# Sandwich layer, one core: three of four heads' probabilities turned by VectorE and moved through DRAM, shared weights resident, one lasting tile for table rows, zeros written one block per step

## The chip, the cores and the metric

The kernel runs on 1 core of one Trainium2 chip. The metric is device time in microseconds (us), the median of 3 runs. A profile of one execution is read beside it. Engines are named as in the profile: PE is TensorE's matmul side and PEld its weight loads, DVE is VectorE, ACT is ScalarE, POOL is GpSimd, and SP is SyncE, which issues most DMAs.

## What is computed

Input x has 8 sequences of 512 rows of 512 numbers, all f32. Two blocks follow each other, each of the form x + norm(block(norm(x))), where norm is a layernorm without weights. The reference, cut to what matters:

```python
c_kv, c_q = x @ W_DKV + b_DKV, x @ W_DQ + b_DQ            # latent 128
k_c, v_c, q_c = c_kv @ W_UK + b_UK, c_kv @ W_UV + b_UV, c_q @ W_UQ + b_UQ
k_r, q_r = (x @ W_KR + b_KR) * pe, (x @ W_QR + b_QR) * pe  # 32 wide, shared by 16 heads
scores = (q_c k_c + q_r k_r) / sqrt(32)                    # 16 heads of 32, per sequence 512 x 512
ctx = softmax(scores) @ v_c;  attention = ctx @ W_O + b_O
# second block: 16 experts, 2 per row by a grouped top-k of sigmoid router scores
routed = sum over chosen e of weight_e * relu(x @ w_up[e])**2 @ w_down[e]   # 512 -> 256 -> 512
shared = relu(x @ shared_up)**2 @ shared_down                               # 512 -> 1024 -> 512
```

## The kernel before

The work has three stages: attention with the shared expert mixed into it, the routed experts, and a tail that adds the parts and normalizes.

**Attention.** The loop at L1094 runs over 8 sequences `b` and 16 steps `g` each. A step is one group of four heads (`m = g // 4`) and one block of 128 query rows (`qt = g % 4`). `scores(b, g)` (L345) makes four score tiles of 128 x 512 on PE. On DVE, one operation per head (L370) adds the position scores, writes the negated sum to SBUF and takes its row minimum. On ACT, L380 makes the exponentials in place. The probabilities have queries on partitions, and the weighted sum with the values needs keys there, so each must be turned. That is done in two ways:

- Heads 0 and 1, tile `p`: `keys_first` (L403) turns each on PE in four 128 x 128 transposes (L410) one step later. The result is copied out of PSUM into `pT`, head 0 by DVE (L418) and head 1 by ACT (L420).
- Heads 2 and 3, tile `pb`: `blocks` (L422) turns 32 x 32 blocks on DVE in one instruction (L427) into `pB`, of which there are two buffers. Four DMAs (L439) write `pB` to one of four DRAM buffers `turned`. In the next step `put_together` (L443) reads it back with one DMA (L446) into the tile `pTb`. The DRAM round trip moves the blocks to their partitions.

`weighted_sum` (L468) runs once per group of four steps, at the second step of the next group (g % 4 == 1), and reads the one `pT` and the one `pTb` tile (L479). The last group of the last sequence is turned wholly on PE.

**What else a step holds.** `beside(b, g)` (L1019) lists the other attention work by step: the output projection of the sequence before (g 2 and 3), its norms, router and top-k (g 4 to 10), the indirect DMAs by POOL that scatter its rows into `table` (`send`, g 11 and 12), and the first projections of the next sequence (g 6 to 15). The rest of a step is filled from the list `waiting`, items of the shared expert with written-out costs, up to BUDGET = 5.4 per step (L1015, L1105). These items begin at step 7 of sequence 1. Thirteen of the sixteen half sequences of the shared expert are done in this stage, three in the tail.

**Order.** PE's order in this stage is the order of the calls. The order on the other engines and on SP is made by a scheduler from dependencies and a model of costs. Each queue is worked off in order, so an instruction that waits holds up those behind it.

**The pieces that the change touches.**

- Shared up weights: in this stage `load_wsu` (L748) reads 512 KB pieces into two buffers `wsu` whenever a piece is due (L752). For the tail the whole 2 MB go into `wsu_all`, loaded in the middle of the routed stage (L976). `shared_down` lies in `wsd` from the start (L194).
- Table rows: `ao[b]` (L504, L541) is one tile per sequence from a pool with one buffer. It holds the attention output, then its normed rows, the 16 expert weights, a row number at NUMBER and 15 zeros. `weights` (L673) writes weights, zeros (the memset at L684) and numbers. Since the buffer is one, a write into the new tile waits for the scatters that read the tile before.
- Zeros: `none` (L113) is a tile of zeros with a row number. `clear(g)` (L731) writes it from SBUF, in sequence 0, three 256 KB blocks of `sums` and one 272 KB block of `table` in each step (L738, L739), 57 DMAs with the one at L195.

**Routed stage.** 79 tiles of 128 table rows, each with the weights of its expert (L880 and on): 272 KB of rows (`xg`) and up to 1 MB of weights per tile, three weight buffers.

Of the kernel before, what the change touches and what calls it, by code (L numbers as in the profile page):

```python
# [38 lines left out]
def sandwich_kernel(  # L39
# [65 lines left out]
    def load_rows(src, b, name):  # L105
        t = sh.tile([P, NT, D], F32, tag="x", name=f"{name}_{b}")
        for i in range(NT):
# [3 lines left out]
    xs, res = {0: load_rows(x, 0, "x")}, {}  # L111

    none = sb.tile([P, W], F32, name="none")  # L113
    nc.vector.memset(none, 0.0)
    nc.gpsimd.iota(none[:, NUMBER : NUMBER + 1], pattern=[[0, 1]], base=T, channel_multiplier=1,
                   allow_small_or_imprecise_dtypes=True)
    numbers = sb.tile([P, B * NT], F32, name="numbers")
# [76 lines left out]
    wsd = chunked(shared_down, "wsd", const)  # L194
    nc.sync.dma_start(table[NE * REGION :, :], none)  # L195
# [123 lines left out]
    def heads(b, m):  # L319
# [18 lines left out]
    rope, probs, pTs, ctxs, dens, wides, last_max = {}, {}, {}, {}, {}, {}, {}  # L338
    BLK = HEAD_DIM
    NB = P // BLK  # L340
    turned = [
        dram.tile([P, NB, 2 * NT * BLK], F32, name=f"turned_{i}") for i in range(NT)
    ]

    def scores(b, g):  # L345
# [3 lines left out]
        tiles, order = {}, (2, 3, 0, 1)  # L349
        for h in order:  # L350
# [10 lines left out]
        pr = [  # L361
            at.tile([P, 2, S], F32, tag="p", name=f"p_{b}_{g}", bufs=2),
            at.tile([P, 2, S], F32, tag="pb", name=f"pb_{b}_{g}"),
        ]
# [3 lines left out]
        for h in order:  # L368
            p_h = pr[h // 2][:, h % 2, :]
# [9 lines left out]
            )  # L379
            nc.scalar.activation(  # L380
# [7 lines left out]
        probs[b, g] = pr  # L388
# [5 lines left out]
    def turned_probs(b, m):  # L394
        if (b, m) not in pTs:
            pTs[b, m] = (
                at.tile([P, 2, NT, S], F32, tag="pT", name=f"pT_{b}_{m}"),

                at.tile([P, NT * NB, 2, NT, BLK], F32, tag="pTb", name=f"pTb_{b}_{m}"),
            )  # L400
        return pTs[b, m]

    def keys_first(b, g, hs):  # L403

        m, qt = divmod(g, NT)
        for h in hs:
            pr = probs[b, g][h // 2][:, h % 2, :]
            pt = ps_o.tile([P, NT, P], F32, tag="o", name=f"pt_{b}_{g}_{h}")
            for c in range(NT):
                nc.tensor.transpose(pt[:, c, :], pr[:, c * P : (c + 1) * P], ident)  # L410
            to = turned_probs(b, m)[h // 2]
            if h < 2:
                to = to[:, h, :, qt * P : (qt + 1) * P]
            else:
                to = to[:, qt * NB : (qt + 1) * NB, h - 2].rearrange("p i c q -> p c i q")
                pt = pt.rearrange("p c (i q) -> p c i q", q=BLK)
            if h % 2 == 0:
                nc.vector.tensor_copy(to, pt)  # L418
            else:
                nc.scalar.copy(to, pt)  # L420

    def blocks(b, g):  # L422


        pr = probs[b, g][1]
        pB = at.tile([P, NB, 2, NT, BLK], F32, tag="pB", name=f"pB_{b}_{g}", bufs=2)
        turn = nc.vector.transpose(  # L427
            pB.rearrange("p j h c q -> p (h c) j q"),
            pr.rearrange("p h (c j q) -> p (h c) j q", j=NB, q=BLK),
        )  # L430
        tc.add_manual_dep(
            turn.ins,
            last_max.pop((b, g)).ins.name,
            mybir.DependencyInfo(mybir.DependencyClass.NoSync, mybir.DependencyReason.SCHED_ONLY),
            reason="the exponentials take a while",
        )
# [6 lines left out]
    def put_together(b, g):  # L443
        m, qt = divmod(g, NT)
        to = turned_probs(b, m)[1][:, qt * NB : (qt + 1) * NB]
        nc.sync.dma_start(to.rearrange("p i h c q -> p i (h c q)"), turned[qt])  # L446
# [12 lines left out]
    def turn_denominators(b, m, pt=None):  # L459
# [5 lines left out]
        ctxs[b, m] = at.tile([P, S], F32, tag="ctx", name=f"ctx_{b}_{m}", bufs=5)  # L465
        nc.scalar.copy(ctxs[b, m], pt.rearrange("p t q -> p (t q)"))

    def weighted_sum(b, m, ps=None):  # L468
# [5 lines left out]
        for c in range(NT):  # L474
            for h in range(4):
# [4 lines left out]
                    to if h < 2 else to.rearrange("p (n q) -> p n q", q=BLK),  # L480
                    lhsT=vs[b][:, c, col : col + HEAD_DIM],
                    rhs=pT[:, h, c, :] if h < 2 else pTb[:, :, h - 2, c, :],
# [17 lines left out]
    ao, xT, sc_, chosen_ = {}, {}, {}, {}  # L500

    def project_out(b, i):
        if i == 0:
            ao[b] = at.tile([P, NT, W], F32, tag="ao", name=f"ao_{b}")  # L504
# [4 lines left out]
        nc.vector.tensor_tensor(ao[b][:, i, 0:D], ps, bo, ALU.add)  # L509
# [6 lines left out]
    def residual(b):  # L516

        rows = [ao[b][:, i, 0:D] for i in range(NT)]
# [7 lines left out]
    def norm_f(b):  # L526
        rstd, off = norm_stats([res[b][:, i, :] for i in range(NT)], f"f{b}")
        for i in range(NT):
            normalize(ao[b][:, i, 0:D], res[b][:, i, :], rstd, off, i)
        del res[b]  # L530

    def turn_f(b, i):
        if i == 0:
            xT[b] = sh.tile([P, NK, S], F32, tag="xT", name=f"xT_{b}", bufs=2)
        turn_rows(ao[b], xT[b], i, f"f{b}")

    def last_sequence(prev, fill):
# [3 lines left out]
        ao[b] = at.tile([P, NT, W], F32, tag="ao", name=f"ao_{b}")  # L541
# [21 lines left out]
        for i in range(NT):  # L563
            ps, row, xb = acc[i], ao[b][:, i, 0:D], res[b][:, i, :]
# [5 lines left out]
        for i in range(NT):  # L570
            turn_rows(ao[b], xT[b], i, f"f{b}")
# [101 lines left out]
    def weights(b):  # L673
        chosen = chosen_[b][1]
        comb = ao[b][:, :, D:NUMBER]
# [5 lines left out]
        nc.vector.tensor_tensor(  # L681
            comb, comb, total.unsqueeze(2).to_broadcast([P, NT, NE]), ALU.mult
        )
        nc.vector.memset(ao[b][:, :, NUMBER + 1 :], 0.0)  # L684
        nc.vector.tensor_copy(
            ao[b][:, :, NUMBER : NUMBER + 1], numbers[:, b * NT : (b + 1) * NT].unsqueeze(2)
        )

# [42 lines left out]
    def clear(g):  # L731


        assert NE == NSTEP
        todo = [(1, c) for c in range(T // P + 1)] + [(0, T // P)]
        todo += [(0, c) for c in range((2 * B - LATE) * NT // 2, B * NT)]
        for i, c in todo[g * 3 : (g + 1) * 3] if g < NSTEP - 1 else todo[g * 3 :]:
            nc.sync.dma_start(sums[i][c * P : (c + 1) * P, :], none[:, 0:D])  # L738
        nc.sync.dma_start(table[g * REGION : g * REGION + P, :], none)  # L739

    def send(b, i):
        for j in range(TOP_K):
            scatter(slots[b][:, i, j : j + 1], ao[b][:, i, :])


    hT, wsu_, ysum = {}, {}, {}

    def load_wsu(b, a, i):  # L748
        if (b, a, i) not in wsu_ and 2 * b + a < 2 * B - LATE:
            wsu = sh.tile([P, NK, INTER], F32, tag="wsu", name=f"wsu_{b}_{a}_{i}", bufs=2)  # L750
# [462 lines left out]
```

## Time and profile before

| | us |
|---|---|
| runs | 1772.99, 1770.25, 1768.58 |
| median | 1770.25 |
| the profiled execution, its own time | 1769.93 |
| its span, first to last instruction | 1768.2 |
| score matmuls of step 0 of sequence 0 begin | 33.4 |
| sequence 0, 16 steps (33.4 to 137.4) | 104.0 |
| sequences 1 to 6 | 162.0, 157.5, 159.1, 159.3, 158.5, 160.2 |
| sequence 7 and what follows, to the first routed tile (1093.9 to 1324.4) | 230.5 |
| routed stage (1324.4 to 1660.0) | 335.6 |
| tail | 108.2 |

The time around the span is 1.7 us. Stage bounds are the starts of instructions on PE's timeline: a sequence begins with the scores of its step 0. The profile gives for each engine its busy time, for each group of instructions a count and a mean duration, and for each idle stretch of an engine who ended it ("<-"). A busy PE is not a PE at its peak: at a granted clock of 0.5 the same matmul takes twice as long and counts as busy.

### The profile page before, as it was taken

To read this page: it belongs to the slowest core of one execution; us is meant where nothing else is said; L and a number is where in the kernel's file an instruction comes from. 1 tells how busy PE (TensorE), PEld (TensorE's weight loads), DVE (VectorE), ACT (ScalarE), POOL (GpSimd) and SP (SyncE) were. 2 spreads that over 40 slices of the span, in tenths; PEclk is the share of its full clock that TensorE was granted. 3 is DMA by queue.
4 is the path that set the end of the run, shared out by engine and by line. 5 is a ranking of instruction groups with operands and counts; after the bars stand their busy time and mean duration, and the time that the engine had idled before them with its cause. 6 is when DMAs were issued, how large, how long until landed. Compare 5 with 4: busy or idle time off the path is not lost. (4 is left out here: it accounts for less than half of the span.)

```text
span 1768.2 us, 25701 instructions
## 1 busy us (share of the span) xinstructions
PE 1602.3 (91%) x8122; PEld 931.8 (53%) x8122; DVE 991.2 (56%) x2929; ACT 820.5 (46%) x1943; POOL 227.9 (13%) x210
## 2 busy tenths in 40 slices
PE   7788789899997998898989989999989998999995
PEld 3333554454554445444554545466457676776663
DVE  3766755765585568457755746775333332333366
ACT  4656645564564556455644645565312222222134
POOL 0000010001000100100010010002013333333222
PEclk9889899989998999898999989999999999999998
DMA  6987574446454645645564566464156978979898
GB/s 202 292 295 221 155 227 129 146 145 224 143 173 140 212 141 177 196 143 151 156 215 129 162 189 185 136 189 155 53 183 129 243 139 201 232 138 288 222 310 171
DMA packets 210728, 324.33 MB, mean 183 GB/s; under 512 B 22945, under 2 KB 126369, under 8 KB 210593
## 3 DMA queue, kind: packets, MB, share of 16 engines
q1 hardware_dynamic: 189696, 275.76, 50.3%
q0 software_dynamic: 20896, 46.93, 13.7%
q8 instruction: 65, 1.06, 0.3%
q14 instruction: 71, 0.57, 0.1%
HBM read 237.93 MB, written 142.36 MB: 215 GB/s over the span
## 5 line engine op out<-in xcount | busy, mean ns | idle before, releaser
L380 ACT ACTIVATE pb<-pb,nmax 128x512 f32<-128x512 f32 x256 | 182.8, 715 | 285.0 <-DVE nmax L370 282.1
L768 PE MATMUL h<-xT,wsu 128*128 128x256 f32 x832 | 214.0, 414 | 57.0 <-DMA wsu<-in_L_ffn_shared_up_dram 40.6
L783 PE MATMUL y<-wsd,hT 128*128 128x512 f32 x512 | 235.2, 609 | 12.1 <-DVE nmax L370 6.4
L370 DVE CUSTOM_DVE_ANT_0 pb<-s,rope 128x512 f32<-128x512 f32 x256 | 167.1, 687 | 132.9 <-PE s L353 131.1
L768 PEld LDWEIGHTS h<-xT,wsu 128*128 128x128 f32 x832 | 170.1, 209 | 99.4 <-issue 24.2
L380 ACT ACTIVATE p<-p,nmax 128x512 f32<-128x512 f32 x256 | 181.2, 709 | 2.0 <-DVE nmax L370 1.7
L410 PEld LDWEIGHTS pt<-ident,p 128*128 128x128 f32 x1024 | 110.3, 141 | 110.8 <-issue 37.2
L926 PE MATMUL hg<-xgT,set_up 128*128 128x128 f32 x1264 | 156.7, 277 | 12.1 <-DMA set_up<-in_L_ffn_w_up_dram 11.8
L370 DVE CUSTOM_DVE_ANT_0 p<-s,rope 128x512 f32<-128x512 f32 x256 | 167.1, 684 | 0.9 <-PE s L353 0.9
L783 PEld LDWEIGHTS y<-wsd,hT 128*128 128x128 f32 x512 | 96.9, 195 | 128.4 <-issue 101.9
L353 PE MATMUL s<-k,q 32*128 32x512 f32 x1024 | 157.5, 657 | 1.0 <-ACT q L329 1.0
L926 PEld LDWEIGHTS hg<-xgT,set_up 128*128 128x128 f32 x1264 | 148.5, 193 | 16.8 <-issue 8.9
L427 DVE STREAM_TRANSPOSE pB<-pb 128x1024 f32<-128x1024 f32 x124 | 153.3, 1236 | 6.1 <-ACT pb L380 4.8
L950 POOL DMA_INDIRECT sums<-y,to x79 | 122.6, 1551 | 236.1 <-DVE y L949 194.9
L410 PE MATMUL pt<-ident,p 128*128 128x128 f32 x1024 | 142.6, 281 | 7.5 <-DVE ctx L486 4.6
L941 PE MATMUL yg<-set_down,hgT 128*128 128x512 f32 x316 | 148.5, 593 | 0.0
L453 POOL COPY wide<-rden 128x512 f32<-128x512 f32 x32 | 19.7, 615 | 905.3 <-DVE rden L451 532.9
L479 PE MATMUL o<-pTb,v 128*32 128x512 f32 x496 | 118.3, 621 | 12.8 <-issue 7.0
L935 DVE TENSOR_TENSOR hgT<-hgT 128x256 f32<-128x256 f32 x79 | 33.6, 425 | 164.4 <-ACT hgT L934 164.4
L479 PE MATMUL o<-pT,v 128*32 128x512 f32 x496 | 120.7, 621 | 0.3 <-DVE pT L418 0.2
L420 ACT COPY pT<-pt 128x512 f32<-128x512 f32 x128 | 72.8, 568 | 102.3 <-PE pt L410 102.3
L911 ACT COPY xgT<-pt_g 128x512 f32<-128x512 f32 x79 | 46.2, 586 | 145.8 <-PE pt_g L909 145.7
(222 smaller groups left out, 2167.7 us busy)
## 6 DMA issues: line engine op xcount, KB each, us to landing
turned<-pB SPq DMA_DIRECT2D x496, 128.0 KB
pTb<-turned SPq DMA_DIRECT2D x124, 512.0 KB
set_up<-in_L_ffn_w_up_dram SPq DMA_DIRECT2D x79, 512.0 KB
set_down<-in_L_ffn_w_down_dram SPq DMA_DIRECT2D x79, 512.0 KB
wsu<-in_L_ffn_shared_up_dram SPq DMA_DIRECT2D x52, 512.0 KB
xg<-table SPq DMA_DIRECT2D x79, 272.0 KB
end<-sums SPq DMA_DIRECT2D x32, 512.0 KB
sums<-none SPq DMA_DIRECT2D x40, 256.0 KB
```

Of the source, the lines that this page charges most:

```text
L353: nc.tensor.matmul(tiles[h], lhsT=q[r0 : r0 + HEAD_DIM, qt * P : (qt + 1) * P], rhs=k[r0 : r0 + HEAD_DIM, :], start=True, stop=True,)
L370: last_max[b, g] = nc.vector.tensor_tensor_reduce(out=p_h, in0=tiles[h], in1=rope[b, qt], scale=-1.0, scalar=3.0e38, op0=ALU.add, op1=ALU.min,
L380: nc.scalar.activation(p_h, p_h, AF.Exp, bias=nmax[:, h : h + 1], scale=-1.0, accum_out=dens[b, m][:, qt, h : h + 1],)
L410: nc.tensor.transpose(pt[:, c, :], pr[:, c * P : (c + 1) * P], ident)
L420: nc.scalar.copy(to, pt)
L427: turn = nc.vector.transpose(pB.rearrange("p j h c q -> p (h c) j q"), pr.rearrange("p h (c j q) -> p (h c) j q", j=NB, q=BLK),)
L479: nc.tensor.matmul(to if h < 2 else to.rearrange("p (n q) -> p n q", q=BLK), lhsT=vs[b][:, c, col : col + HEAD_DIM], rhs=pT[:, h, c, :] if ...
L768: nc.tensor.matmul(ps[:, 0:HALF], lhsT=wsu[:, k, :], rhs=xT[b][:, k, a * HALF : (a + 1) * HALF], start=(k == 0), stop=(k == NK - 1),)
L783: nc.tensor.matmul(ysum[c], lhsT=hT[b][:, i, t * P : (t + 1) * P], rhs=wsd[:, i, :], start=(i == 0), stop=(i == NH - 1),)
L926: nc.tensor.matmul(ph[:, i * P : (i + 1) * P], lhsT=sets[j % NBUF][0][:, k, i * P : (i + 1) * P], rhs=xgT[j][:, k, :], start=(k == 0), sto ...
L941: nc.tensor.matmul(py, lhsT=hg[j][:, i * P : (i + 1) * P], rhs=sets[j % NBUF][1][:, i, :], start=(i == 0), stop=(i == NI - 1),)
L950: nc.gpsimd.indirect_dma_start(out=sums[j % 2][:, :], out_offset=bass.IndirectOffsetOnAxis(ap=to[j], axis=0), in_=y, in_offset=None, compu ...
```

## The change

- Heads 1, 2 and 3 (NV = 3) are turned by DVE and moved through DRAM, head 0 (NP = 1) by PE. The DVE turn is two instructions, of two heads and of one. `turned` rows grow from 1 KB to 1.5 KB, and `pTb` from 512 KB to 768 KB per step. The PE-turned head is copied by ACT, and DVE's copy goes. `pB` has one buffer in place of two.
- Hints to the scheduler (`in_order`; no wait on the chip comes of them by themselves): a step's row minima come after the step before's turn on DVE. The row number is written after the weights. A block of zeros comes after the step's `put_together`.
- `wsu` (2 MB) and `wsd` (2 MB) are both loaded in sequence 0, in steps 6 and 9, and stay. All sixteen halves of the shared expert read them. `load_wsu` and `wsu_all` are gone.
- `ao` is one lasting tile; its zeros are written once, at the start, by POOL. The memset in `weights` is gone.
- `none` is a short-lived tile that shares `pB`'s buffer. It is written to the last rows of `table`, and the zeros are copied from there, DRAM to DRAM. `clear` is a generator that gives one block per step from sequence 1 on (56 blocks, to step 7 of sequence 4).

The diff, cut:

```diff
+    BLK = HEAD_DIM
+    NB = P // BLK
+    NV = 3
+    NP = 4 - NV
-    none = sb.tile([P, W], F32, name="none")
+    none = at.tile([P, NB, NV, NT, BLK], F32, tag="pB", name="none")
+    none = none.rearrange("p j h c q -> p (j h c q)")[:, 0:W]
...
+    nc.sync.dma_start(table[NE * REGION :, :], none)
+    none = table[NE * REGION :, :]
+
+    ao = at.tile([P, NT, W], F32, name="ao")
+    nc.gpsimd.memset(ao[:, :, NUMBER + 1 :], 0.0)
...
-    wsd = chunked(shared_down, "wsd", const)
-    nc.sync.dma_start(table[NE * REGION :, :], none)
+    wsd = const.tile([P, NH, D], F32, name="wsd")
+    wsu = const.tile([P, NK, HID], F32, name="wsu")
...
-        tiles, order = {}, (2, 3, 0, 1)
+        tiles, order = {}, [*range(NP, 4), *range(NP)]
...
+            if last_turn:
+                in_order(last_max[b, g], last_turn[-1], "transfers wait for it")
...
-            if h % 2 == 0:
+            if (NP - 1 - h) % 2 == 0:
+                nc.scalar.copy(to, pt)
+            else:
                 nc.vector.tensor_copy(to, pt)
-            else:
-                nc.scalar.copy(to, pt)
...
-        pr = probs[b, g][1]
-        pB = at.tile([P, NB, 2, NT, BLK], F32, tag="pB", name=f"pB_{b}_{g}", bufs=2)
-        turn = nc.vector.transpose(
-            pB.rearrange("p j h c q -> p (h c) j q"),
-            pr.rearrange("p h (c j q) -> p (h c) j q", j=NB, q=BLK),
-        )
+        pb, last = probs[b, g][1], last_max.pop((b, g))
+        pB = at.tile([P, NB, NV, NT, BLK], F32, tag="pB", name=f"pB_{b}_{g}")
+        for h in range(0, NV, 2):
+            hs = slice(h, min(h + 2, NV))
+            turn = nc.vector.transpose(
+                pB[:, :, hs].rearrange("p j h c q -> p (h c) j q"),
+                pb[:, hs].rearrange("p h (c j q) -> p (h c) j q", j=NB, q=BLK),
+            )
+            in_order(turn, last, "the exponentials take a while")
+        last_turn.append(turn)
...
-        nc.vector.memset(ao[b][:, :, NUMBER + 1 :], 0.0)
...
+    def load_shared():
+        for w, src in ((wsu, shared_up), (wsd, shared_down)):
+            yield nc.sync.dma_start(w, src.rearrange("(c p) n -> p c n", p=P))
...
-            if j == NTILES // 2:
-                nc.sync.dma_start(wsu_all, shared_up.rearrange("(c p) n -> p c n", p=P))
...
-                    keys_first(*prev, range(2))
+                    keys_first(*prev, range(NP))
                     if by_vector(prev[0], prev[1] // NT):
-                        put_together(*prev)
+                        moved = put_together(*prev)
...
-                if b == 0:
-                    clear(g)
+
+                if (b > 0 or g in (6, 9)) and moved is not None:
+                    for ins in itertools.islice(spare, 1):
+                        in_order(ins, moved, "others are waited for")
```

## The prediction

> **What bounds the kernel now.** I read the table by stages first, then who waited for whom on PE and DVE, then the groups, then the timeline at each stall. Columns of the table by stages: stretch and its length, then busy time (and instructions) of PE, PEld, DVE, ACT, POOL, the granted clock, the DMA share, GB/s. The rows are sequence 0, sequence 4 and the routed stage.
>
> ```profile
> 33.40:137.40 104.00, 83.06 (x453) 36.87 (x452) 73.11 (x174) 66.43 (x164) 1.84 (x3) 0.89 0.83 269
> 616.00:775.20 159.20, 147.24 (x733) 77.79 (x732) 100.92 (x280) 86.29 (x208) 10.23 (x12) 0.95 0.54 168
> 1324.40:1660.00 335.60, 317.49 (x1896) 233.51 (x1895) 110.35 (x382) 77.08 (x159) 119.47 (x77) 0.99 0.85 196
> ```
>
> Sequence 4 stands for sequences 1 to 6: PE is busy 147 of 159 us, DVE 101, ACT 86, DMA at half. PE sets the pace there, so less PE work and fewer PE stalls count in full. Sequence 0 has no shared expert to fill it; PE has the most busy time but waits, and the DMA share is 0.83.
>
> The waits of PE and DVE (total us, times, longest):
>
> ```profile
> PE h L768 <- DMA wsu<-in_L_ffn_shared_up_dram: 40.6, 6, 9.0
> PE h L768 <- DVE nmax L370: 13.8, 3, 5.0
> PE y L783 <- DVE nmax L370: 6.4, 1, 6.4
> DVE ao L684 <- DMA table<-ao,slots: 73.4, 7, 12.8
> ```
>
> PE loses 40.6 us to shared up weights that come late. The fourth line explains the second and third. The memset of the new `ao` tile waits for the scatters of the old one, at the head of DVE's queue; the row minima stand behind it, and PE runs out of free PSUM tiles:
>
> ```profile
> 424.01 0.11 DVE L684 MEMSET ao<- 128x60 f32 x1 [10.47 <-DMA table<-ao,slots]
> ...
> 425.16 5.18 PE L768 MATMUL h<-xT,wsu 128*128 128x256 f32 x16 [4.02 <-DVE nmax L370]
> ```
>
> The clock shows what a stall costs after it ends. Table by stages around the 7.8 us weight stall at 345.9:
>
> ```profile
> 345.90:353.70 7.80, 0.03 (x4) 0.00 (x0) 7.77 (x22) 4.98 (x13) 0.00 (x0) 0.74 0.76 264
> 353.70:359.90 6.20, 6.14 (x20) 3.12 (x24) 2.19 (x8) 3.70 (x7) 0.00 (x0) 0.50 0.36 98
> 359.90:367.00 7.10, 7.10 (x64) 4.26 (x56) 4.71 (x13) 2.01 (x4) 0.00 (x0) 1.00 0.71 241
> ```
>
> For 6.2 us after the stall the clock is 0.50: half of that time is lost as well.
>
> **The change, part by part.** The sum is made against the profiled execution, 1769.9 us (span 1768.2 and 1.7 around it), 0.3 us under the median, 1770.25.
>
> *PE transposes.* One head less per step is turned on PE. PE's timeline and the group:
>
> ```profile
> 45.27 1.09 PE L410 MATMUL pt<-ident,p 128*128 128x128 f32 x8
> 46.20 0.59 PE L327 MATMUL ps_k<-ckv,w_uk 128*128 128x512 f32 x1
> ...
> L410 PE MATMUL pt<-ident,p 128*128 128x128 f32 x1024 | 142.6, 281 | 7.5 <-DVE ctx L486 4.6
> ```
>
> Eight transposes delay the next matmul by 0.93 us, start to start (the mean of 281 ns overlaps its neighbours), so four cost 0.46 us. 124 steps lose four; the 16 of sequence 0 are not PE-bound and go into the term below; 108 x 0.464 = **-50 us**. The last group keeps four heads on PE.
>
> A rule of the Trainium skill speaks against this move: "VectorE: DVE Perf Modes", section "Rules for kernel authors", gives 128 x 128 transposes to TensorE if the result may lie in PSUM, and VectorE only those within 32 x 32 blocks. Its section "The three transpose paths" has 390 ns on TensorE and 311 on VectorE for 128 x 128 in bf16; 432 transposes (108 x 4) at 390 ns would be an estimated 168 us. The start-to-start row above says 50, so the row decides.
>
> *DVE and ACT.* DVE's turn of two heads takes 1236 ns, so three take 1.85 us (+0.62 per step); its copy L418 of 685 ns goes. That is nothing on balance, on an engine at 63% in sequence 4. ACT copies one head as before.
>
> *Weight stalls.* `wsu` stays on chip. Five stalls in sequences 2 to 6 go: 7.8 + 9.0 + 6.1 + 7.7 + 8.9 = **-39 us** (a sixth, 1.2 us at 1306, is left out). What is late next there is PE's own work: in the 7.8 us stall DVE and ACT were already waiting for it.
>
> *The memset.* Six PE stalls stand where DVE waited for scatters: 6.4 (at 261), 4.0, 1.6, 5.0, 4.8, 0.9 = **-23 us**. `project_out` still writes `ao` after the scatters, but five steps later.
>
> *Clock after these stalls.* The 0.5 stretches that outlast nine of them: 3.7 + 6.2 + 3.0 + 4.8 + 3.7 + 4.5 + 4.8 + 5.0 + 3.3 = 39 us, half lost: **-19 us**.
>
> *Routed stage.* The 2 MB load of `wsu_all` is issued at 1486.0; PE then waits 5.7 us for rows at 1493.7 (of 6.0 in the whole stage), and 4 us at 0.5 follow: **-8 us**. The stage is otherwise PE-bound and unchanged, as is the tail.
>
> *Sequence 0.* 55 of the 56 clears and the 9.4 us stall on late rows of x (86.7) leave; 15 MB at 269 GB/s were 55 us of DMA. But its steps are a chain: the turn (1.85 us), four issues and the landing. From the turn's end to the read of `turned` the quiet case took 3.4 us for 512 KB:
>
> ```profile
> 433.88 1.24 DVE L427 STREAM_TRANSPOSE pB<-pb 128x1024 f32<-128x1024 f32 x1
> ...
> 435.15 1.76 SPq L439 DMA_DIRECT2D turned<-pB  x4
> 438.48 0.84 SPq L446 DMA_DIRECT2D pTb<-turned  x2
> ```
>
> I take 4.2 us for 768 KB: half of 1.6 us of landing more. With one `pB` the next turn waits for this landing: a cycle of 6.1 us. Once a group the weighted sum lies in it too, since SP has the read of `pTb` that waits for the sum ahead of the next write. That makes some 25 us a group, 100 for four. The two 2 MB loads stand in the same queue, 6.6 us each at the 317 GB/s of the `wsu_all` stall: 113 against 104. Bounds: -16 (6.95 and 9.4 us of stalls gone, chain hidden) and +15. I take **+5**, between them, as the first group starts without a backlog.
>
> *The new wait: one `pB`.* In sequences 1 to 7 the turn at the head of DVE's queue waits for the landing of the step before. Behind it stand the row minima and the squares of the shared expert; PE waits for both. The turns there end 9.86 us apart on average, 107 distances, 13 of them under 7 us. Each shortened by 0.46 us and held to a cycle c, they lose in all 6.5 us at c = 6.1, 17 at 7, 45 at 8, 87 at 9, 149 at 10. These are upper bounds, since a late DVE catches up in a long step. The clears and the larger moves take about 35 MB per sequence in 142 us, 246 GB/s, near sequence 0's 269; a write often lies behind a 768 KB read. I take c = 7: **+17**, bounds 0 and 87.
>
> Here too a rule speaks against the change: "DMA: Bandwidth & Descriptors", section "Latency and other measured facts", gives HBM access 0.2 us on average and 2 us at high load. The quiet case above shows no more than 1.6 us of landing; adding 1.8 would make c 7.9, cost 41 us instead of 17 and end at an estimated 1680.
>
> *SP's new waits.* The clears of steps 11 and 12 in sequences 1 to 3 read `table` and so wait on SP for four scatters each, 1.27 us apart on POOL; the reads and writes of the turned heads queue behind them. Scatters took 6.4 us to land. The read is needed two steps later: **+3**, bounds 0 and 6 x 6.4 = 38.
>
> Sum: -50 - 39 - 23 - 19 - 8 + 5 + 17 + 3 = -114: **1656 us**.
>
> **The rivals.**
> - *More comes back.* The cycle stays near 6.1 us (+6) or hides wholly, sequence 0 gains 10, SP's waits vanish: -50 - 39 - 23 - 19 - 8 - 10 + 6 = -143: 1627. For it: DVE is 37% idle. Against: the two engines wait for each other in turns. 18%.
> - *Half goes into the cycle.* Landing slows to 6 or 7 us, c = 8 to 9: +45 to +87 instead of 17, 1684 to 1726. For it: in sequence 0, at share 0.83, turn end to read took 7.9 and 8.3 us with clears or a load of x between. Against: that queue held 1 MB of clears per step; now it is 256 KB. 18%.
> - *Slower: the cycle becomes the bound.* Gains without the +17 are 131, so c decides from 9.8 us, where the loss is 135: a landing of 7.9 us in every step, what sequence 0 shows in its worst. At c = 10.5 the loss is 189: 1828. 6%.
> - *It doesn't do what it says.* The scheduler puts another waiting instruction at the head of DVE's or SP's queue, and stalls of the same length take the place of those removed. Only transposes and the routed stage gain: 1770 - 50 - 8 + 20 = 1732. 5%.
>
> **How the numbers follow.** The forecast, 1635 to 1680, has 53%. The range of 8 in 10 reaches from 1612 to 1715: the first rival below, most of the second above; the third, the fourth and the top of the second are left out, about 15%. About 0.3%, 5 us, can be told from no change. Slower comes from the third rival, 6%; no change is a sliver between it and the fourth, 2%; faster 92%.
>
> **What would show each step.** Right: sequences 2 to 6 take 136 to 146 us each; no wait for `wsu` on PE, none for scatters on DVE of over 5 us; PE has some 560 transposes of probabilities in place of 1056; the routed stage takes 326 to 329 us with no row stall of 5 us; DVE's waits for `turned` sum to under 60 us. Wrong: sequences 1 to 7 near 160 us with DVE idle before the turns (the second or third rival), or long PE waits for DVE with another name behind them (the fourth). Sequence 0 over 120 us would say that the chain was underrated.

## The result and the profile after: ten per cent slower

| | us |
|---|---|
| changed kernel, runs | 1945.8, 1953.2, 1953.7, 1964.5 |
| median | 1953.45 |
| kernel before, beside it | 1771.62 |
| ratio | 1.103, 95% interval 1.097 to 1.109 |
| profiled execution, its own time and span | 1964.54, 1962.8 |

The profiled execution is the slowest of the four, 11 us over the median, so small terms are not read from it. The forecast was 1656; the outcome lies beyond even the rival of the other side, 1828.

By stages (columns as in the prediction: stretch and length, busy time and instructions of PE, PEld, DVE, ACT and POOL, granted clock, DMA share, GB/s): sequence 0, sequence 4 and the routed stage.

```profile
34.10:160.90 126.80, 90.18 (x394) 35.37 (x394) 67.71 (x162) 66.07 (x160) 1.84 (x3) 0.77 0.67 209
708.20:894.00 185.80, 151.74 (x670) 74.20 (x670) 104.50 (x287) 91.12 (x216) 10.91 (x13) 0.89 0.63 189
1520.50:1854.00 333.50, 316.39 (x1894) 233.49 (x1893) 109.33 (x381) 76.93 (x159) 119.46 (x77) 0.99 0.84 191
```

Sequence 4 takes 186 us, not 159 and not the 136 to 146 that were forecast. No compute engine is fuller than before: PE is busy 152 of 186 us (147 of 159 before), DVE 104.5 (101 before). The DMA share rose from 0.54 to 0.63. The granted clock fell from 0.95 to 0.89. From the first score matmul to the first routed tile the stage grew from 1291.0 to 1486.8 us; the routed stage and the tail did not grow by as much as 1 us. Who waited (total us, times, longest):

```profile
PE o L497 <- DMA pTb<-turned: 97.9, 17, 9.9
DVE pB L449 <- DMA turned<-pB: 94.0, 38, 7.9
PE pt L430 <- ACT p L393: 41.4, 13, 7.8
```

The waits for `wsu` on PE and for the scatters on DVE are gone, as forecast. In their place PE waits for `pTb` at the weighted sum, in 23 of 31 groups for more than 2 us (2 before). One such wait, step 1 of sequence 4, on the timeline of all engines (start, duration, engine, line):

```profile
712.58 0.34 SPq L464 DMA_DIRECT2D pTb<-turned  x1
...
716.86 0.43 DVE L784 TENSOR_TENSOR hT<-hT 128x256 f32<-128x256 f32 x1 [1.30 <-ACT hT L783]
717.20 1.83 DVE L449 STREAM_TRANSPOSE pB<-pb 128x1024 f32<-128x1024 f32 x2
...
719.06 2.23 SPq L457 DMA_DIRECT2D turned<-pB  x4
...
724.10 0.34 SPq L464 DMA_DIRECT2D pTb<-turned  x1
...
728.45 1.07 PE L497 MATMUL o<-pTb,v 128*32 128x512 f32 x3 [7.73 <-DMA pTb<-turned]
```

From the start of the turn to the weighted sum takes 11.3 us. The surprise is the first two lines. The read at 712.58 shows that the writes of the step before had landed, so the one `pB` was free, and the exponentials had ended at 711.0. The turn starts at 717.2 all the same: it stands in DVE's queue behind squares of the shared expert, which wait for PE by way of ACT. PE in turn comes to wait for this turn. Step 2 of the same sequence shows it with other work:

```profile
741.60 0.34 SPq L464 DMA_DIRECT2D pTb<-turned  x1
...
743.21 0.69 DVE L526 TENSOR_TENSOR ao<-ps_ao,bo 128x512 f32<-128x512 f32 x1 [1.51 <-PE ps_ao L603]
...
746.64 0.69 DVE L526 TENSOR_TENSOR ao<-ps_ao,bo 128x512 f32<-128x512 f32 x1 [1.79 <-PE ps_ao L603]
...
748.30 1.84 DVE L449 STREAM_TRANSPOSE pB<-pb 128x1024 f32<-128x1024 f32 x2
```

Here `pB` is free at 741.6 and the exponentials are done at 742.1, and the turn starts 6.2 us later, behind two additions that wait for PE's output projection. Summed over the kernel, 123 turns stand 331 us behind other DVE work with both inputs ready. From the end of the exponentials of the DVE heads to the turn it takes 5.1 us on average, 0.83 before.

What PE lost: its idle time before the routed stage grew by 139 us, from 116.6 to 255.8. Of that, 126 us lie before the weighted sums, which the page's groups show (busy us, mean ns of one matmul, idle us before); first the kernel before, then the changed one:

```profile
L479 PE MATMUL o<-pTb,v 128*32 128x512 f32 x496 | 118.3, 621 | 12.8 <-issue 7.0
```

```profile
L497 PE MATMUL o<-pTb,v 128*32 128x512 f32 x744 | 160.6, 807 | 138.6 <-DMA pTb<-turned 97.9
```

PE's busy time grew too, from 1174.6 to 1231.2 us, although its transposes fell from 137.4 to 86.4 (each matmul counted without what overlaps the one before it). The weighted sums grew from 121.1 to 187.7, since they run just after a stall, at a low clock. The wait shown above lies in the second of these stretches; in the 4.3 us after it the granted clock was 0.53:

```profile
708.20:718.00 9.80, 8.59 (x45) 5.96 (x44) 4.24 (x12) 5.89 (x15) 0.68 (x1) 1.00 0.69 191
718.00:738.00 20.00, 12.27 (x53) 3.98 (x52) 10.49 (x24) 8.58 (x21) 0.00 (x0) 0.74 0.64 190
```

The scores grew from 148.2 to 172.3 us, but not by the clock: one of their matmuls takes 666 ns on average, 657 before. The eight of a step overlap less: they are spread over more than 1.4 us in 38 steps of 128, in 13 before.

### The profile page after: what moved, and what is told of

Read it like the earlier page. It is cut to its first block, busy times and chain, and to the rows that moved or that the text cites. A ratio compares the mean times of both kernels' runs of the same rounds, so it can differ in the third digit from the quotient of the medians.

```text
span 1962.8 us, 24570 instructions
## 1 busy us (share of the span) xinstructions
PE 1659.0 (85%) x7626; PEld 912.3 (46%) x7626; DVE 999.7 (51%) x2921; ACT 829.7 (42%) x1943; POOL 228.6 (12%) x211
## 5 line engine op out<-in xcount | busy, mean ns | idle before, releaser
L393 ACT ACTIVATE pb<-pb,nmax 128x512 f32<-128x512 f32 x384 | 271.5, 710 | 32.2 <-DVE nmax L381 32.1
L449 DVE STREAM_TRANSPOSE pB<-pb 128x1024 f32<-128x1024 f32 x248 | 227.5, 956 | 103.7 <-DMA turned<-pB 94.0
L497 PE MATMUL o<-pTb,v 128*32 128x512 f32 x744 | 160.6, 807 | 138.6 <-DMA pTb<-turned 97.9
L776 PE MATMUL h<-xT,wsu 128*128 128x256 f32 x1024 | 254.1, 406 | 8.2 <-DVE nmax L381 4.3
L381 DVE CUSTOM_DVE_ANT_0 pb<-s,rope 128x512 f32<-128x512 f32 x384 | 244.5, 686 | 26.3 <-PE s L363 25.1
L393 ACT ACTIVATE p<-p,nmax 128x512 f32<-128x512 f32 x128 | 92.1, 720 | 192.2 <-DVE nmax L381 192.0
L497 PE MATMUL o<-pT,v 128*32 128x512 f32 x248 | 167.0, 818 | 0.0
L784 DVE TENSOR_TENSOR hT<-hT 128x256 f32<-128x256 f32 x128 | 53.2, 425 | 185.2 <-ACT hT L783 181.2
L430 PEld LDWEIGHTS pt<-ident,p 128*128 128x128 f32 x512 | 56.7, 146 | 145.1 <-ACT p L393 62.5
L430 PE MATMUL pt<-ident,p 128*128 128x128 f32 x512 | 88.5, 298 | 41.4 <-ACT p L393 41.4
```

The costliest lines, as they stand in the source:

```text
L381: last_max[b, g] = nc.vector.tensor_tensor_reduce(out=p_h, in0=tiles[h], in1=rope[b, qt], scale=-1.0, scalar=3.0e38, op0=ALU.add, op1=ALU.min,
L393: nc.scalar.activation(p_h, p_h, AF.Exp, bias=nmax[:, h : h + 1], scale=-1.0, accum_out=dens[b, m][:, qt, h : h + 1],)
L449: turn = nc.vector.transpose(pB[:, :, hs].rearrange("p j h c q -> p (h c) j q"), pb[:, hs].rearrange("p h (c j q) -> p (h c) j q", j=NB, q ...
L497: nc.tensor.matmul(to if h < NP else to.rearrange("p (n q) -> p n q", q=BLK), lhsT=vs[b][:, c, col : col + HEAD_DIM], rhs=pT[:, h, c, :] i ...
L776: nc.tensor.matmul(ps[:, 0:HALF], lhsT=wsu[:, k, i * P : (i + 1) * P], rhs=xT[b][:, k, a * HALF : (a + 1) * HALF], start=(k == 0), stop=(k ...
```

## Experiments

All medians and ratios to the kernel before, which ran beside each set (1772 to 1777 us):

| run | heads by DVE, `pB` buffers | us | ratio (95%) |
|---|---|---|---|
| changed kernel | 3, 1 | 1953 | 1.103 (1.097 to 1.109) |
| e1_pb2 | 3, 2 | 1814 | 1.022 (1.019 to 1.025) |
| e2_turn_first | 3, 1 | 1932 | 1.087 (1.084 to 1.091) |
| e3_two_heads | 2, 1 | 1692 | 0.954 (0.949 to 0.958) |
| e4_two_heads_pb2 | 2, 2 | 1689 | 0.952 (0.949 to 0.955) |
| e5_read_first | 3, 2 | 1829 | 1.033 (1.029 to 1.037) |
| e6_read_turn_first | 3, 2 | 1887 | 1.064 (1.061 to 1.067) |
| e7_no_hint | 3, 1 | 1940 | 1.094 (1.091 to 1.097) |
| e8_third_head_alone | 3, 2 | 1901 | 1.071 (1.068 to 1.074) |
| e9_sp_by_call | 3, 2 | 1826 | 1.030 (1.025 to 1.034) |
| e10_sp_dve_by_call | 3, 2 | 1890 | 1.064 (1.060 to 1.069) |
| e11_two_heads_sp | 2, 1 | 1708 | 0.962 (0.958 to 0.967) |
| e12_two_thirds | 3, 2 | 1677 | 0.944 (0.942 to 0.946) |
| e13_two_pb | 3, 2 | 1821 | 1.025 (1.022 to 1.027) |
| e14_light_order | 3, 2 | 1727 | 0.975 (0.971 to 0.979) |
| e15_heavy_order | 3, 2 | 1758 | 0.991 (0.988 to 0.993) |
| e16_one_pb_light_order | 3, 1 | 1758 | 0.990 (0.987 to 0.993) |
| e17_one_pb_lighter_order | 3, 1 | 1755 | 0.989 (0.988 to 0.991) |
| e18_two_heads_light_order | 2, 1 | 1712 | 0.965 (0.963 to 0.966) |

The scheduler that orders DVE, ACT, SP and POOL is called the planner here. The built kernel shows the order that it made. "Lag" is the time from the last exponential of a step's DVE heads to the step's turn, on average: 0.8 us before, 5.1 in the changed kernel. Between a step's minima and its turn stand on average 1.1 other DVE instructions in the kernel before and 5.9 in the changed one; more than three stand there in 6 and in 47 of 124 steps.

### Which part of the change

Two buffers of `pB` for the changed kernel:

```diff
-        pB = at.tile([P, NB, NV, NT, BLK], F32, tag="pB", name=f"pB_{b}_{g}")
+        pB = at.tile([P, NB, NV, NT, BLK], F32, tag="pB", name=f"pB_{b}_{g}", bufs=2)
...
-    wdq, bdq = chunked(w_dq, "wdq", at), column(b_dq, "bdq")
+    wdq, bdq = wdkv, column(b_dq, "bdq")
...
-    wqr, bqr = rope_weights(w_qr, b_qr, "qr")
+    wqr, bqr = wkr, bkr
...
+    wuv = wuk
```

> The changed kernel with two buffers of pB again (to make room, three weight tiles are shared: the query latent uses the key latent's weights, the value up weights are the key's, the rotary query weights the rotary key's; so the output has other values, with the same instructions but three small loads less). Theory A, the turn stands late in DVE's queue because it is planned to wait for the one pB: the turn starts about 1 us after the exponentials instead of 5.1 us on average, sequences 2 to 6 take 140 to 150 us instead of 175 to 186, 1650 to 1700 us in all. Rival B, three heads by DRAM are too long a chain whatever the buffers: PE goes on waiting 4 to 8 us once a group for pTb, 1880 us or more. Rival C, the zeros from DRAM to DRAM and SP's queue delay the transfers: 1880 us or more, with the turn near the exponentials but reads that land late.

Measured 1814: 140 us better than the changed kernel, and still slower than before. The lag fell to 0.8 us, as theory A (late turns because of the one `pB`) said, but the time did not follow to 1650 or 1700: PE still idles 84 us before the weighted sums, 13 before the change. Rivals B and C, 1880 or more, missed the time too. Late turns are a part; the third head must cost by other ways too.

DVE's order, by hints on every DVE instruction that is called after the turn:

```diff
+                dve.behind = last_turn[-1] if by_vector(b, g // NT) else None
                 for cost, f in now + more:
                     f()
+                dve.behind = None
```

> The changed kernel with one pB, with the DVE work that is called after the turn of a step also ordered behind it in DVE's queue (hints to the scheduler alone, no wait on the chip). Theory A: most of the 331 us that the turns stand behind other DVE work with their inputs ready goes, the time from the last exponential to the turn falls from 5.1 to 2 or 3 us; since one pB still holds every turn until the landing of the one before, 1720 to 1820 us. Rival B: the order on DVE does not matter, 1930 to 1970 us. Rival C: the same, 1930 to 1970.

Measured 1932, where rivals B and C had it. The turns do come earlier (a lag of 2.0 us), and PE's idle time before the weighted sums falls from 138.6 to 36.1 us. But what was pushed behind the turns is now late, and PE waits for that instead:

```profile
PE pt_a L277 <- ACT x L269: 91.6, 8, 18.2
...
PE pt_f L277 <- ACT ao L269: 76.3, 7, 11.5
...
PE ps_pos L729 <- DVE cum L100: 48.5, 7, 9.0
```

These are the norms' transposes and the router's counts; the first wait was 35.6 us in the changed kernel, and its list has neither of the others. A turn put first by this rule moves the wait elsewhere.

Two heads by DVE, one line (e4_two_heads_pb2 has the edit of e1_pb2 as well):

```diff
-    NV = 3
+    NV = 2
```

> The changed kernel with two heads turned by DVE (NV = 2) and one pB; resident weights, lasting ao, zeros one per step stay. In the planned order 24 of 124 turns stand behind more than three other DVE instructions, against 47 in the changed kernel and 6 in the kernel before. Theory A: half way, 1730 to 1820 us. Rival B (three heads are the cause): 1660 to 1700 us, the gains of the rest without the loss. Rival C (zeros, SP): 1880 or more.

> Two heads by DVE and two buffers of pB (three weight tiles shared as in the first kernel of this call): what is left of the change is resident weights, lasting ao and zeros one per step. Theory A and rival B: 1770 - 39 - 23 - 19 - 8 = 1681, so 1660 to 1700 us. Rival C: 1800 or more.

Measured 1692 and 1689: rival B, that three heads are the cause, had the time. Everything in the change but the third head is worth 82 to 85 us, and with two heads one `pB` costs 3 us at most in the sum. (The second kernel also shares three small weight tiles; the pair shows both together.) Sequence 4 of the one-buffer kernel runs on PE, at full clock:

```profile
587.80:731.00 143.20, 141.20 (x737) 74.14 (x736) 100.47 (x280) 85.96 (x208) 10.35 (x13) 1.00 0.60 184
```

So the third head costs 1953 - 1692 = 262 us as it stands in the change, and 1814 - 1689 = 125 us with two buffers. The third head alone, in the kernel before:

```diff
+    NV, NP = 3, 1
...
-        tiles, order = {}, (2, 3, 0, 1)
+        tiles, order = {}, (1, 2, 3, 0)
...
-        pB = at.tile([P, NB, 2, NT, BLK], F32, tag="pB", name=f"pB_{b}_{g}", bufs=2)
+        pB = at.tile([P, NB, NV, NT, BLK], F32, tag="pB", name=f"pB_{b}_{g}", bufs=2)
```

> The kernel before with three heads turned by DVE and nothing else of the change: two buffers of pB, the clears in sequence 0, weights in pieces, no new hints (one buffer less for ctx, four as in the changed kernel, to make room). Theory D: its reads too stand behind the next step's first write in 70 of 93 cases inside groups, so PE waits for pTb as in e1_pb2, which lost 125 us against two heads: 1820 to 1900 us. Rival C, the loss needs the zeros moved one per step beside the heads: 1720 to 1770 us.

Measured 1901, 125 us over the kernel before and just over what theory D expected, but not by the wait that it named. The lag is 0.4 us, and PE waits for the pieces of `wsu`, which share SP's queue with the turned heads, 141.6 us in place of 40.6:

```profile
PE h L772 <- DMA wsu<-in_L_ffn_shared_up_dram: 141.6, 18, 18.0
```

So the clears beside the heads (rival C) are not needed for a loss of this size.

### One queue at a time: no

Theory D was that single places in the planned queues cost the time. With two buffers the read of a step stood on SP behind the first write of the next step, so that it waited for the next turn. A hint puts it first; a second kernel adds e2's hints on DVE:

```diff
-            nc.sync.dma_start(
+            write = nc.sync.dma_start(
                 to[i], pB[i * BLK : (i + 1) * BLK].rearrange("k j h c q -> k j (h c q)")
             )
+            if moved is not None and g % NT != 1:
+                in_order(write, moved, "the read before is waited for")
```

> Three heads and two buffers of pB (weight tiles shared as in e1_pb2), with a hint that puts the four writes of a step behind the read of the step before on SP; before, the read of steps 1 and 3 of a group stood behind the first write of the next step in 30 of 31 groups, and so waited for the next turn. Theory D, the planned order on SP and DVE is what costs: PE's waits for pTb fall from 78 us to under 25, 1690 to 1770 us, since 29 of 124 turns still stand behind more than three other DVE instructions. Rival B, the transfer of three heads is too long in itself (turn 1.85, four issues 2.2, landing 2.8, read some 4.5, together 11.3 us): 1790 to 1830 us, no change.

> The same, and DVE's work that is called after a turn is ordered behind it too. Theory D: the third head's gain of 108 x 0.464 = 50 us comes out, 1640 to 1720 us. Rival B: 1790 us or more. If DVE's work that PE waits for (norms, sums for the router) comes late behind the turns, as it did with one pB, 1720 to 1800 us.

Measured 1829 and 1887, against 1814 without, as rival B expected. The second has a lag of only 0.4 us, and PE idles 120 us before the weighted sums all the same. The planner kept the hint and put other transfers between the writes and the read. SP's timeline in e5_read_first, steps 3 to 5 of sequence 4:

```profile
699.80 2.22 SPq L456 DMA_DIRECT2D turned<-pB  x4
702.06 0.85 SPq L760 DMA_DIRECT2D table<-table  x1
711.84 1.67 SPq L530 DMA_DIRECT2D out_dram<-res  x2
713.70 0.33 SPq L465 DMA_DIRECT2D pTb<-turned  x1
```

SP sits from 702.9 to 711.8 before a transfer of rows out that needs DVE's sum. The read stands behind it; by the 2.7 us that writes took to land elsewhere (below), it could have gone at an estimated 704.7. SP's queue in the order of the calls, then DVE's too:

```diff
-    with tc.manual_schedule(engines={mybir.EngineType.PE}):
+    with tc.manual_schedule(engines={mybir.EngineType.PE, mybir.EngineType.SP}):
```

> Three heads, two buffers of pB (weight tiles shared as in e1_pb2), and SP's queue in the order of the calls in the attention stage: the read of a step, then the writes of the next, then x rows, output rows, zeros. In e1_pb2 and e5_read_first the planner put other transfers (rows out that wait for DVE) between the writes and the read that needs them, up to 9 us where the writes had landed after 3. Theory D (the planned queues cost, not the transfers): 1700 to 1770 us, with PE's waits for pTb under 40 us; what remains late is DVE's order (28 turns of 124 behind more than three others). Rival B (the transfer of three heads is too long in itself): 1800 to 1840 us.

> The same with DVE's queue in the order of the calls as well: minima of a step, on one step of four the product with the weighted sum, the turn, then the rest. Theory D: the turn starts within 1 us of the exponentials in three steps of four; 1640 to 1740 us, unless DVE waits for ScalarE within the norms, which by the calls nothing else fills, some 2 us in each of 4 steps of a sequence, 60 us in all. Rival B: 1800 us or more.

> Two heads, one buffer of pB, the rest of the change, and SP's queue in the order of the calls. With two heads the planned order is good already (1692 us), so theory D expects little: 1670 to 1710 us. Rival B says nothing other.

The last is e3_two_heads with SP so. Measured 1826, 1890 and 1708 (16 more than with the planned order). In this form theory D fell: no queue, put in order by a simple rule, gives the time back. The hint of the change itself, that the minima follow the turn before:

```diff
-            if last_turn:
-                in_order(last_max[b, g], last_turn[-1], "transfers wait for it")
```

> The changed kernel without the hint that puts a step's minima behind the turn of the step before (in the planned order 33 turns of 124 then stand behind more than three others, against 47). Theory A/D: the minima of the heads that DVE turns must wait for that turn in any case, since they overwrite the tile that it reads, so only head 0's minimum moves: 1880 to 1950 us. A rival, that the hint is the cause: 1700 to 1830 us.

Measured 1940: it is not the cause. PE's wait of 41.4 us for ACT's `p` shrank to 3.2, but its wait before the transposes of the denominators (`pt_d`) grew from 20.2 to 63.8.

### Volume, or the tie between minima and turn

```diff
+    MOVED = 2
...
-        dram.tile([P, NB, NV * NT * BLK], F32, name=f"turned_{i}") for i in range(NT)
+        dram.tile([P, NB, MOVED * NT * BLK], F32, name=f"turned_{i}") for i in range(NT)
...
-                    rhs=pT[:, h, c, :] if h < NP else pTb[:, :, h - NP, c, :],
+                    rhs=pT[:, h, c, :] if h < NP else pTb[:, :, min(h - NP, MOVED - 1), c, :],
```

> Three heads turned by DVE, two buffers of pB (weight tiles shared as in e1_pb2), but only two of the three heads' blocks are written to DRAM and read back (128 KB and 512 KB in place of 192 and 768); the weighted sum takes the second head's tile twice, so the fourth head's part of the output is not its own. DVE's and PE's work is that of three heads. Theory V, the volume moved (or what the planner makes of it: with it the planned order puts no other DVE work between minima and turn in 110 of 124 steps) is the cost: 1630 to 1690 us, the transposes' gain of some 50 us on top of e4_two_heads_pb2. Theory K, three of four heads in the one tile pb tie each step's minima to the turn before and that is the cost: 1780 to 1830 us, as e1_pb2.

For the other, `pb` gets a second buffer, room is made, and the hint of e7_no_hint goes:

```diff
-        pb = at.tile([P, NV, S], F32, tag="pb", name=f"pb_{b}_{g}")
+        pb = at.tile([P, NV, S], F32, tag="pb", name=f"pb_{b}_{g}", bufs=2)
...
-    wsd = const.tile([P, NH, D], F32, name="wsd")
+    wsd = wsu.rearrange("p k n -> p (k n)").rearrange("p (h d) -> p h d", d=D)
```

> Three heads, two buffers of pB and two of pb, full volume, no hint on the minima (for room, weight tiles shared as in e1_pb2, and the down weights of the shared expert are the up weights' tile, so one load of 2 MB less). Theory K: minima no longer wait for the turn before; 1640 to 1720 us. Theory V: 1770 to 1830 us, as e1_pb2.

Measured 1677 and 1821. Theory K, that three heads in the one tile `pb` tie the minima to the turn before, falls in both. With a third less volume the third head's loss is gone. But less volume changes two things: the transfers, and what the planner makes of them (0.4 other instructions between minima and turn, against 2.7 in e1_pb2).

### Transfers or orders: two by two

The orders of DVE, ACT, SP and POOL of one kernel can be laid upon another by a chain of hints, since both issue the same instructions under the same names:

```diff
+        for chain in CHAINS:
+            names = [f"I-{i}" for i in chain if f"I-{i}" in made]
+            for a, b in zip(names, names[1:]):
+                tc.add_manual_dep(made[b].ins, a, NO_SYNC_SCHED_ONLY, reason="a given order")
```

(`CHAINS` holds the instruction numbers of the attention stage in the other kernel's order, `made` the instructions by name; the dependency's kind is written short here.)

> Three heads, two buffers of pB, full volume as in e1_pb2 (1813 us), with the orders of DVE, ACT, SP and POOL taken instruction by instruction from e12_two_thirds (1677 us), as hints to the scheduler. Theory P, the planner's orders for transfers that it takes for too long are the cost, and the transfers themselves fit: 1680 to 1730 us. Theory T, the transfers themselves take too long on the chip: 1790 us or more.

> The reverse: two thirds of the volume moved as in e12_two_thirds, with the four orders of e1_pb2. Theory P: 1780 to 1820 us. Theory T: 1680 to 1720 us.

| us | orders planned for the full volume | orders planned for two thirds |
|---|---|---|
| full volume moved | 1814 (e1_pb2) | 1727 (e14_light_order) |
| two thirds moved | 1758 (e15_heavy_order) | 1677 (e12_two_thirds) |

Theory P (the orders) and theory T (the transfers) are each half right, and the two effects add up: the orders cost 87 or 81 us, the transfers 55 or 50. That they add up also says that a foreign order has no visible price of its own in these four. Where the transfers cost is seen by sequences. Sequence 2, with a block of zeros in every step, and sequence 5, without zeros; first e14_light_order, then e12_two_thirds:

```profile
303.30:460.00 156.70, 142.69 (x689) 74.73 (x688) 101.72 (x283) 87.47 (x212) 10.21 (x12) 0.93 0.72 228
766.20:909.00 142.80, 135.49 (x686) 71.64 (x685) 101.30 (x283) 87.35 (x212) 10.46 (x12) 0.99 0.72 221
```

```profile
280.20:427.60 147.40, 139.35 (x688) 74.41 (x687) 101.61 (x283) 87.48 (x212) 10.43 (x12) 0.95 0.60 184
716.40:860.70 144.30, 138.70 (x685) 73.95 (x684) 101.21 (x283) 87.46 (x212) 10.46 (x12) 0.95 0.54 160
```

Without zeros the full volume costs nothing (142.8 against 144.3, and 144.9 against 145.1 in sequence 6); with them it costs 9.3 us in sequence 2, 7 to 10 in each of sequences 1 to 4, and 16 in sequence 0, which has the two loads of 2 MB in the same queue. The mean DMA share is 0.72 in both rows of the full volume, so it is no matter of the mean. But the zeros are not all of it. In sequences 1 to 3 the cost lies in the first four and the last four steps (1.7 to 5.4 us each); the eight steps between, with zeros too, differ by at most 0.4 us per four. In sequence 4 the zeros end after eight steps, and 8.1 of its 10.2 us lie in the first four. That the zeros lie ahead of a read in the DMA queues, in steps that also have other transfers, is the likely way; no run without zeros was made, and it stays argued.

### The one buffer, with better orders

The same chain of hints on the changed kernel and on e3_two_heads, with orders that the planner made for less volume:

> The changed kernel itself (one pB, full volume, its own weights) with the orders that the planner makes for it when two thirds of the volume are moved (25 of 124 turns behind more than three others in place of 47). Theory P: the two causes stay apart, the one pB goes on holding each turn until the landing before it: 1750 to 1850 us. Theory T: 1930 us or more.

> The changed kernel itself (one pB, full volume, its own weights) with orders that the planner makes for it when only one of the three heads is moved: 108 of 124 turns directly behind the minima, as in e14_light_order, which had two buffers of pB and 1727 us. If the buffer matters only by what the planner makes of it: 1720 to 1750 us. If the one pB has a price of its own: 1770 us or more, since a turn that stands first waits at DVE's head for the landing before it.

> Two heads and one pB as in e3_two_heads (1692 us), with the orders that the planner makes when one of the two heads is moved (5 turns of 124 behind more than three others, in place of 24). Theory P: some of the order's cost is left there too, 1670 to 1692 us; if e3 had none, 1690 to 1710 us.

Both kernels with one buffer and three heads come to 1755 to 1758 us, with two different orders. The changed kernel has the same instructions as they have, so it loses 198 us by the orders alone. PE's idle time before the weighted sums, 138.6 us in the changed kernel, is mostly gone in e17_one_pb_lighter_order:

```profile
L840 PE MATMUL o<-pTb,v 128*32 128x512 f32 x744 | 123.8, 644 | 28.2 <-DMA pTb<-turned 14.9
```

The lag alone does not decide: with 2.7 us e16_one_pb_light_order takes 1758, with 2.0 us e2_turn_first takes 1932. The chains set four queues at once, and which of them counts most was not told apart. Against two buffers (1727) some 29 us remain for the buffer, between the two forecasts; the orders of the two are not the same, so that figure is rough. The waits of the turn for the landing before it, one buffer (e17_one_pb_lighter_order) and two (e14_light_order):

```profile
DVE pB L420 <- DMA turned<-pB: 198.3, 61, 10.9
```

```profile
DVE pB L420 <- DMA turned<-pB: 15.4, 6, 6.0
```

DVE waits more than in the changed kernel (94.0) and the whole is 198 us faster: a wait at the head of a queue counts by what is behind it and who needs that, not by its length. The kernel with two heads gains nothing: 1712 with orders planned for lighter transfers, 1692 with its own. An order planned for another kernel can have its own price, 20 us here.

## Why the prediction was wrong, by its own steps

**The step that failed** is "The new wait: one `pB`". It took c = 7 us for turn, issues and landing, and let the turn start as soon as `pB` is free, in the place that it had in DVE's queue before. The cycle itself was about right. Where the read is the next transfer on SP, the writes landed 2.7 us after the last issue in the median (1.6 before); with 2.2 us of issues and the 1.85 us turn that is 6.8. But the turn did not start when `pB` was free, since the planner had put other work ahead of it: 5.9 instructions on average, and a lag of 5.1 us. "A late DVE catches up" was the wrong way round: PE, which should have given the long steps, came to wait for the turn. The prediction took the order of the queues as it was before; the orders planned anew are the largest item. In place of the +17 for the wait and the -50 for the transposes the third head cost 262 us, on this way from kernel to kernel:

| from | to | us |
|---|---|---|
| e3_two_heads, 1692 | e12_two_thirds, 1677: a third head, good orders, no more volume (and two buffers, worth 3 at most) | -15 |
| e12_two_thirds | e14_light_order, 1727: its volume | +50 |
| e14_light_order | e17_one_pb_lighter_order, 1755: one buffer (rough) | +29 |
| e17_one_pb_lighter_order | changed kernel, 1953: the orders planned for it | +198 |

**Transposes, -50.** The size was right as busy time and wrong as a gain. Attention stage of e4_two_heads_pb2, then of e12_two_thirds:

```profile
33.80:1245.00 1211.20, 1155.84 (x5860) 622.13 (x5860) 801.01 (x2275) 690.05 (x1670) 82.14 (x96) 0.97 0.55 167
```

```profile
32.00:1229.50 1197.50, 1108.88 (x5363) 574.53 (x5363) 798.77 (x2275) 688.69 (x1670) 83.00 (x96) 0.95 0.55 169
```

PE is busy 47 us less, and the stage is 14 us shorter: 33 us come back as idle time, 28 of them where PE waits for rows that DVE and ACT normalize. First e4, then e12:

```profile
PE pt_a L253 <- ACT x L245: 15.4, 5, 9.9
PE pt_f L253 <- ACT ao L245: 7.7, 1, 7.7
```

```profile
PE pt_a L254 <- ACT x L246: 24.8, 7, 10.5
PE pt_f L254 <- ACT ao L246: 26.5, 5, 9.1
```

With the step shorter by 0.46 us the next limit was close behind, and the prediction had not asked for it. The rule against this move, which gives 128 x 128 transposes to TensorE (the Trainium skill's "VectorE: DVE Perf Modes", section "Rules for kernel authors"), had the right side here: the best kernel that moves three whole heads takes 1727 us, with two heads it is 1689. It was not for DVE's time, which is 801 us with two heads and 799 with three.

**Weight stalls, memset, clock and routed stage, -89 in all:** right in sum. Two heads with the rest of the change measured -82 and -85, with +4 and -6 of sequence 0 in them. One reading was wrong: in the 7.8 us weight stall DVE was not waiting for PE; the prediction's own row has it busy 7.77 of them. The stall went all the same. The routed stage, to its last matmul, gave 1.3 to 5 us of its 8 (336.5 before; 335.2 and 331.7): the wait for rows went, and waits for `set_up` grew from 11.8 to some 15.

**Sequence 0, +5:** it took 126.8 us, +23, beyond the upper bound of +15. With two heads it is 108.1 with one buffer and 98.4 with two, so the chain was underrated both for the third head and for the one buffer.

**SP's waits for scatters, +3:** 18.8 us in three waits on SP; what they cost in the sum was not told apart from the rest.

**The rivals.** The third had the right side by luck, with the wrong mechanism: a cycle of 10.5 us, while the measured one is about 7; the turns stand 11.4 us apart on average (9.86 before) since they start late. The fourth named the mechanism ("puts another waiting instruction at the head of DVE's or SP's queue") and priced it by the stalls that go. A stall that a queue order makes has no reason to be as long as the ones that it replaces.

**What stays open:** why the planner orders so much worse at 768 KB than at 512 KB. That it takes the transfers for longer than they are would fit, and is not shown. Nor did a run put the weighted sum a step later, which would give the round trip more time under any order.

## What to carry to other kernels

When a buffer count or a transfer's size changes, a scheduler may reorder every queue. Lay the old and the new order of the engine that feeds the transfer side by side and count what stands between an instruction's last input and the instruction, before pricing the wait itself. Moving one instruction forward by a rule is not the cure: of the runs with three heads, whole orders helped much and single rules little or not at all. A mixed change is taken apart first by its boldest part: one constant (two heads in place of three) turned 1953 into 1692 us, and the kernel with it beats both. The Trainium skill's "Trainium Kernel Development and Optimization", section "Best Practices", asks for double buffers to overlap DMA with compute; here the second buffer was worth 140 us under the planned orders, about 29 under better ones and at most 3 with two heads.

## What was not expected of the hardware

Three heads' round trip fits where no zeros move: at 221 GB/s and a DMA share of 0.72 sequence 5 of e14_light_order ran at a clock of 0.99. And the low clock after a stall hits whatever waited: here the weighted sum stands behind the stalls of 23 groups, its mean matmul went from 621 to 807 ns, and it alone took 67 us more (121.1 to 187.7).
